# A two-layer graph network in rounds of gathers: x split beside its first product, degrees as bf16 products, filler by a load model

## The chip, the cores and the metric

The kernel runs on one core of one Trainium2 chip. Its time is the device time in microseconds (us) of one execution; the figure before is the median of three runs, 3415.57 us (3411.55 to 3430.43). One further execution was recorded by the hardware profiler; it took 2910.6 us, of which 2908.8 lie between the first and the last instruction of the trace (the span).

A core has five instruction streams: PE (TensorE, matmuls; its weight loads are listed as PEld), DVE (VectorE), ACT (ScalarE), POOL (GpSimd, used here to issue indirect gathers) and SP (SyncE, used here to issue all other transfers).

## The reference

12,500 nodes with 256 features each, 200,000 edges sorted by their target `dst`. Two convolutions take the mean over the incoming edges, then a linear layer, a residual and a layer norm:

```python
def _sage_conv(x, src, dst, W_l, b_l, W_r):
    msgs = x[src]
    agg = jax.ops.segment_sum(msgs, dst, num_segments=N_NODES)
    deg = jax.ops.segment_sum(jnp.ones((src.shape[0],), x.dtype), dst, num_segments=N_NODES)
    mean = agg / jnp.maximum(deg, 1.0)[:, None]
    return mean @ W_l + b_l + x @ W_r

h = jax.nn.relu(_sage_conv(x, src, dst, W1_l, b1, W1_r))
h = jax.nn.relu(_sage_conv(h, src, dst, W2_l, b2, W2_r))
x = _layernorm(x + h @ W3 + b3)
```

All in f32. `dst` is skewed: it is 12,500 times the square of a uniform number, so nodes with a low index have many edges and the later ones few.

## The kernel before

The nodes are cut into 98 blocks of 128. Each layer has two ways of summing over edges, and runs them beside each other.

**Hot nodes, by dense products.** The first nodes, in groups of 256 (5 groups in layer 1, 7 in layer 2), are not gathered. For each group `count` builds a matrix that says how often each of the 12,500 sources points to each of the 256 targets: bf16, 128 x 98 x 256. Per tile of 128 edges DVE makes the picks (L661) and, for four tiles, `low` (L665) and `aft` (L671); PE multiplies them (L691 for the first 128 tiles, L706 and L710 later), and DVE (L697) or ACT (L712) puts the result into `counts`. `product` (L628) then multiplies the matrix with x. x is kept as three bf16 parts whose sum is x; one load brings `rows`, the parts of two blocks (384 KB), and each block takes six matmuls (L638), 588 for a group. In layer 1 `degrees` (L728) also multiplies the counts by a column of ones. Counts made in layer 1 are written to HBM (`stored`) and read back in layer 2 (`loaded`).

**The split of x.** `split_rows` (L622) loads a block of x in f32 (`split_sb`, L833), `exact` makes the three parts (ACT casts L617 and L619, DVE subtractions L618 and L620, the last cast and difference written as bf16 `parts`), and a store puts them into `x3_d` in HBM (L626). The 98 splits run beside the count of group 0; the products of layer 1 read `x3_d` back.

**Cold edges, by rounds of gathers.** The other edges are taken in rounds of four tiles. Each round issues four indirect gathers on POOL (L243), 128 rows each, into one of four `got` buffers; DVE makes the selection matrices `one` (L201) and `two` (L207); PE multiplies them with the gathered rows (L254 into `part_ps`); ACT copies that out as `some` (L259); PE spreads it over 128 nodes (L265); DVE adds it (L277) to `sums`, a ring of eight blocks. In layer 1 the gathered rows carry a column of ones, so column 256 of `some` counts edges; a one-row f32 matmul (L270) spreads it and DVE adds it (L273) to `degs`, a ring too. Layer 1 has 186 groups of tiles, of which 83 take two rounds: 269 rounds with 1076 gathers. Layer 2 has 247 rounds with 988.

**Finished blocks.** When all edges of a block are summed, `first_block` (layer 1, three pieces) turns x (two transposes L839, ACT copy L842), makes the mean and the two products (`sage`, L863 and L865, DVE L868 and L869, ACT L871), clears its place in the rings (L894 for `sums`, L895 for `degs`), writes h to HBM (L896), splits h with `exact` and writes the parts (L899). The degrees of a block lie as a row of 128 numbers and are needed as a column: a matmul of that row with a single one (L886) turns it, the ACT copy takes it along, and DVE makes max and reciprocal (L889, L890). `last_block` (layer 2, five pieces) is the same with W3, residual and layer norm behind it.

**The order.** `layer` (L562) writes the order out by hand: per round one step of gathers, then three parts, each with at most one piece of a block and a share of the dense work, the filler. The filler is a generator that yields costs; `mixed` weaves the parts of a stage (a count, the product of the group before, a store) together and scales their costs to the largest plus 0.3 of the rest. Each round is given an equal share of the whole cost, until eight rounds before the end. The order on PE and POOL is this order; a scheduler sets that of DVE, ACT and SP from it.

The lines that set the share:

```python
        for i in range(i0, n + 1):
            before = gathers.step()
            due = dense_cost * min(1.0, (i + 1 - i0) / (n - i0 - 8))
            for part in range(3):
                ...
                pieces()
                fill(spent + (due - spent) / (3 - part))
```

Of the kernel before, what the change touches and what calls it, by code (L numbers as in the profile page):

```python
# [1 line left out]

# [19 lines left out]
P = 128  # L22
# [25 lines left out]
def by_runs(  # L48
# [79 lines left out]
    h3_d = dram.tile([P, NB, 3, D], BF16, name="h3_d")  # L128
    count_d = dram.tile([HG1 - 1, P, NB, DN], BF16, name="count_d")
# [86 lines left out]
    class Gathers:  # L216
# [45 lines left out]
        def summed(self, gr, some, two, done):  # L262
# [6 lines left out]
            if self.width > D:  # L269
                nc.tensor.matmul(sum_ps[0:1, NC], lhsT=some[:, D:D + 1], rhs=two,  # L270
                                 start=True, stop=True)
                deg = degs[:, bass.ds(n0, P)]
                nc.vector.tensor_add(deg, deg, sum_ps[0:1, NC])  # L273
# [288 lines left out]
    def layer(gathers, block, n_pieces, dense, dense_cost):  # L562
# [26 lines left out]
        filler = dense(waiting)  # L589
# [8 lines left out]
        begun = gathers.hot // P  # L598
        for i in range(i0, n + 1):
            before = gathers.step()  # L600
            due = dense_cost * min(1.0, (i + 1 - i0) / (n - i0 - 8))
            for part in range(3):
# [6 lines left out]
                fill(spent + (due - spent) / (3 - part))  # L609
# [11 lines left out]

    def split_rows(b):  # L622
        t = load_rows(x, N, b, "split_sb")
        s = work.tile([P, 3, D], BF16, name="parts")
        exact(t, s, t)
        nc.sync.dma_start(x3_d[:, b], s)  # L626

    def product(g, table3, c_sb):  # L628

        ps = dense_pool.tile([P, NC, DN], F32, name="dense_ps")  # L630
        nc.tensor.matmul(ps, lhsT=zeros_b, rhs=c_sb[:, :NC, :DN], start=True, stop=False)
        for b in range(NB):
            if b % 2 == 0:
                rows = work.tile([P, 2, 3, D], BF16, name="rows", bufs=3)
                nc.sync.dma_start(rows, table3[:, b:b + 2])
# [5 lines left out]
            yield COST_DENSE  # L641
# [4 lines left out]
    def count(g, to):  # L646
# [32 lines left out]
        for t in range(lo_g, highs[g]):  # L679
# [6 lines left out]
            if t < FIRST:  # L686
# [13 lines left out]
                yield count_cost(t)  # L700
            else:
                n0 = off_act.at(t)
                for a, b in halves:
# [10 lines left out]
                    yield count_cost(t) / len(halves)  # L714
# [7 lines left out]
    def degrees(g, c_sb):  # L722
# [3 lines left out]
        for j in range(DN // P):  # L726
            for b in range(NB):
                nc.tensor.matmul(ps[:, 0, j:j + 1], lhsT=c_sb[:, b, j * P:(j + 1) * P], rhs=ones_b,  # L728
                                 start=b == 0, stop=b == NB - 1)
                if b % 14 == 13:  # L730
                    yield COST_DEGREES
# [5 lines left out]
    COST_DENSE, COST_DEGREES, COST_SPLIT = 0.7, 1.6, 0.8  # L737
# [8 lines left out]
    def mixed(*parts):  # L746

        costs = [c for _, c in parts]
        scale = (max(costs) + 0.3 * (sum(costs) - max(costs))) / sum(costs)
        left = [[what, c, 0.0] for what, c in parts]  # L750
        while left:
            p = min(left, key=lambda p: p[2] / p[1])
            cost = next(p[0], None)
            if cost is None:
                left.remove(p)
            else:
                p[2] += cost
                yield cost * scale

    def stored(g, c_sb):  # L760
        for b0 in range(0, NB, 14):
            nc.sync.dma_start(count_d[g, :, b0:b0 + 14], c_sb[:, b0:b0 + 14, :DN])
            yield 0.5

    def loaded(g, c_sb):
        for b0 in range(0, NB, 14):
            nc.sync.dma_start(c_sb[:, b0:b0 + 14, :DN], count_d[g, :, b0:b0 + 14])
            yield 0.5

    def dense(g, table3, c_sb, waiting, with_deg):  # L770
        for p in product(g, table3, c_sb):
# [4 lines left out]
        if with_deg:  # L776
            yield from degrees(g, c_sb)
# [3 lines left out]
    def splits():  # L781
        for b in range(NB):
            split_rows(b)
            yield COST_SPLIT

    D_1 = NB * COST_DENSE + DN // P * (NB // 14) * COST_DEGREES
    D_2 = NB * COST_DENSE
    MOVED = NB // 14 * 0.5
    assert NB % 14 == 0 and HG == HG1 + 2

    def stages_1(waiting):

        for g in range(HG1 + 1):
            parts = [(count(g, counts[g % 2]), counting(g))]
            if g == 0:
                parts.append((splits(), NB * COST_SPLIT))
            else:
                parts.append((dense(g - 1, x3_d, counts[(g - 1) % 2], waiting, True), D_1))
                if g < HG1:
                    parts.append((stored(g - 1, counts[(g - 1) % 2]), MOVED))  # L800
            yield list(parts)

    def stages_2(waiting):

        order = [HG1 - 1, HG1, HG1 + 1, *range(HG1 - 1)]
        for i, g in enumerate(order):
            parts = [(dense(g, h3_d, counts[(HG1 - 1 + i) % 2], waiting, False), D_2)]
            if 1 <= i < HG - 1:
                n = order[i + 1]
                to = counts[(HG1 + i) % 2]  # L810
                parts.append((count(n, to), counting(n)) if n > HG1 else (loaded(n, to), MOVED))
            yield parts

    def staged(stages):
        def run(waiting):
            for parts in stages(waiting):
                yield from mixed(*parts)
        return run

    def cost_of(stages):  # L820
        whole = 0.0
        for parts in stages([]):
            costs = [c for _, c in parts]
            whole += max(costs) + 0.3 * (sum(costs) - max(costs))
        return whole
# [10 lines left out]
    def transposed(t, ps, name, more=0):  # L836

        for c in range(NC):
            nc.tensor.transpose(ps[:, c], t[:, c * P:(c + 1) * P], ident)  # L839
        s = work.tile([P, NC * P + 1], F32, name=name)  # L840
        n = NC * P + more
        nc.scalar.copy(s[:, :n], ps.rearrange("p c l -> p (c l)")[:, :n])  # L842
        return s[:, :NC * P].rearrange("p (c l) -> p c l", l=P), s[:, NC * P:]
# [34 lines left out]
    def first_block(b, agg=None):  # L878
        x_sb = load_rows(x, N, b, "x_sb")
        of_ring = agg is None  # L880
        yield True
        ps = turned()
        if of_ring:
            overlap(b, True)
            agg, deg_row = ring(b)
            nc.tensor.matmul(ps[:, NC, 0:1], lhsT=deg_row, rhs=ones[0:1, 0:1], start=True, stop=True)  # L886
        x_t, deg = transposed(x_sb, ps, "own_t", int(of_ring))
# [3 lines left out]
        yield True  # L891
# [426 lines left out]
```

## Time and profile before

| | before |
|---|---|
| median of 3 runs | 3415.57 us (3411.55 to 3430.43) |
| profiled execution | 2910.6 us |
| span of its trace | 2908.8 us |
| mean granted TensorE clock | 0.914 |
| dense products L638 on PE | 7056 matmuls, 976.9 us, 279 ns each |
| gathers L243 on POOL | 1076 and 988 |
| one-row degree products L270 | 186 |
| splits of x: load L833 to store L626 | 98 |
| loads of `rows` in layer 1 and 2 | 245 and 343, 384 KB each |
| HBM traffic | 582.80 MB read, 89.87 MB written |

The profiled execution is shorter than the runs that were timed, by a factor of 1.173. Profile and timed runs are therefore compared each with their own kind.

Engine rows of the profile give busy time, share of the span and number of instructions. Rows of groups give, for one line of the code, engine and shape, the number of instructions, the busy time and the mean of one in ns, then the engine's idle time just before them and what ended most of it. "issue" there is time in which the engine waited for nothing that the profile shows. L numbers are lines of the kernel before.

### The profile page before, as it was taken

What the parts mean: (1) busy time and instruction counts of PE and PEld (TensorE: products, weight loads), DVE (VectorE), ACT (ScalarE), POOL (GpSimd) and SP (SyncE); (2) the same over time, 40 slices, a digit from 0 to 9 for tenths busy, and PEclk for the clock granted to TensorE, in tenths of its full rate; (3) what the DMA queues carried; (4) which work ended last, traced back from release to release, by engine and by line L of the source; (5) the groups of instructions that cost most, each with busy time, mean ns of one, the idle gap of its engine ahead of it and who ended that gap; (6) DMA issues with size and microseconds to landing.
All of it is one profiled execution on the core that took longest, in us unless ns stands there. A gap on an engine that the chain in (4) does not pass through costs nothing.

```text
span 2908.8 us, 54100 instructions
## 1 busy us (share of the span) xinstructions
PE 2394.6 (82%) x18630; PEld 1632.6 (56%) x18630; DVE 1471.2 (51%) x4350; ACT 1253.6 (43%) x2702; POOL 2065.3 (71%) x2074
## 2 busy tenths in 40 slices
PE   3475755898998999999996677877889898899995
PEld 1132323565665666666764455555666666677774
DVE  6687764664554565566564124434323333444443
ACT  0422764675675676677673014444112122222222
POOL 5777764777777777777774777777777777777772
PEclk9676767998999999999998899889999999999998
DMA  4455668877877878767864677777989989888872
GB/s 124 128 174 164 198 188 271 260 232 235 277 228 247 273 227 292 248 215 225 251 203 124 214 246 231 219 220 230 296 284 305 299 287 291 276 265 266 266 251 71
DMA packets 408133, 676.44 MB, mean 233 GB/s; under 512 B 59659, under 2 KB 266537, under 8 KB 407849
## 3 DMA queue, kind: packets, MB, share of 16 engines
q1 hardware_dynamic: 303415, 400.51, 42.5%
q0 software_dynamic: 99072, 270.66, 30.5%
q8 instruction: 149, 2.44, 0.3%
q10 hardware_dynamic: 5362, 1.72, 0.3%
q14 instruction: 135, 1.11, 0.1%
HBM read 582.80 MB, written 89.87 MB: 231 GB/s over the span
## 4 chain that ended last, share of the span: by engine, by line
PE 54%; DMA 19%; POOL 8%; issue 7%; DVE 6%; ACT 4%; DVEq 0%; SPq 0%; ACTq 0%; POOLq 0%
PE dense_ps L638 19%; POOL got L243 8%; PE part_ps L254 7%; PE block_ps L863 6%; DMA got<-h_d,src_t 5%; PE count_ps L706 5%; PE block_ps L865 5%; PE sum_ps L265 4%; DMA x_sb<-in_x_dram 3%; DMA rows<-h_d 3%; DMA rows<-x_d 3%; PE block_ps L839 2%; PE block_ps L921 2%; DMA split_sb<-in_x_dram 2%; PE sum_ps L270 2%
## 5 line engine op out<-in xcount | busy, mean ns | idle before, releaser
L243 POOL DMA_INDIRECT got<-in_x_dram,src_t x1076 | 1116.7, 1038 | 446.5 <-issue 274.2
L243 POOL DMA_INDIRECT got<-h_d,src_t x988 | 946.4, 958 | 343.1 <-issue 285.3
L638 PE MATMUL dense_ps<-counts,rows 128*128 128x256 bf16 x7056 | 976.9, 279 | 51.3 <-DMA rows<-h_d 27.7
L712 ACT CAST counts<-count_ps 128x392 f32 (+2 forms) x1052 | 717.6, 682 | 290.2 <-PE count_ps L710 174.0
L638 PEld LDWEIGHTS <-rows 128*128 128x128 bf16 x7056 | 671.3, 100 | 287.5 <-issue 88.6
L254 PE MATMUL part_ps<-got,one 128*32 128x257 f32 (+1 forms) x4128 | 359.7, 422 | 192.1 <-DMA got<-h_d,src_t 123.0
L706 PE MATMUL count_ps<-pick,low 128*128 128x392 bf16 (+2 forms) x1052 | 343.4, 354 | 57.0 <-ACT counts L712 27.0
L661 DVE TENSOR_SCALAR pick<-steps,key_t 128x686 bf16<-128x686 f16 (+2 forms) x748 | 301.4, 413 | 127.6 <-PE count_ps L706 110.2
L201 DVE TENSOR_TENSOR one<-lo_t,lane_b 128x128 f32<-128x128 bf16 x516 | 149.1, 289 | 372.7 <-PE part_ps L254 370.5
L259 ACT COPY some<-part_ps 128x257 f32<-128x257 f32 (+1 forms) x361 | 136.1, 377 | 431.4 <-PE part_ps L254 428.2
L254 PEld LDWEIGHTS part_ps<-got,one 128*32 128x32 f32 x4128 | 85.9, 111 | 323.5 <-issue 176.4
L265 PE MATMUL sum_ps<-two,some 128*128 128x128 f32 x1444 | 238.2, 290 | 0.2 <-DVE sums L277 0.2
L265 PEld LDWEIGHTS sum_ps<-two,some 128*128 128x128 f32 x1444 | 205.0, 201 | 20.5 <-issue 8.7
L277 DVE TENSOR_TENSOR sums<-sums,sum_ps 128x256 f32 x361 | 148.4, 411 | 132.6 <-PE sum_ps L265 101.9
L868 DVE TENSOR_TENSOR own<-block_ps,biases 128x256 f32<-128x256 f32 x196 | 83.0, 423 | 230.9 <-PE block_ps L865 230.2
L706 PEld LDWEIGHTS <-low 128*128 128x128 bf16 x1052 | 101.8, 100 | 152.3 <-DVE pick L661 54.2
L842 ACT COPY own_t<-block_ps 128x256 f32<-128x256 f32 (+1 forms) x294 | 110.0, 375 | 123.7 <-PE block_ps L839 121.2
L871 ACT ACTIVATE h<-own 128x256 f32<-128x256 f32 x196 | 81.4, 415 | 179.3 <-DVE own L869 179.2
L665 DVE TENSOR_TENSOR low<-low_t,lane_b 128x512 bf16<-128x512 bf16 x187 | 127.9, 684 | 21.1 <-PE count_ps L710 20.5
L710 PE MATMUL count_ps<-aft,low 128*128 128x98 bf16 x614 | 131.9, 215 | 0.0
L863 PE MATMUL block_ps<-w1l_sb,sums 128*128 128x256 f32 x352 | 113.9, 452 | 2.1 <-DVE sums L277 1.8
L863 PE MATMUL block_ps<-w2l_sb,sums 128*128 128x256 f32 x336 | 104.1, 437 | 11.3 <-DVE sums L277 11.1
(180 smaller groups left out, 2495.1 us busy)
## 6 DMA issues: line engine op xcount, KB each, us to landing
rows<-h_d SPq DMA_DIRECT2D x343, 384.0 KB
rows<-x_d SPq DMA_DIRECT2D x245, 384.0 KB
count_d<-counts SPq DMA_DIRECT2D x28, 896.0 KB
counts<-count_d SPq DMA_DIRECT2D x28, 896.0 KB
x_sb<-in_x_dram SPq DMA_DIRECT2D x194, 128.0 KB
x_d<-parts SPq DMA_DIRECT2D x98, 192.0 KB
h_d<-parts SPq DMA_DIRECT2D x98, 192.0 KB
got<-in_x_dram,src_t POOLq DMA_INDIRECT x1076
```

What stands on the lines that cost most here:

```text
L201: nc.vector.tensor_tensor(one, lo[:, a:a + n * (G - 1) + 1:n].unsqueeze(2).to_broadcast([P, G, W]), lane_b[:, :W].unsqueeze(1).to_broadcas ...
L243: nc.gpsimd.indirect_dma_start(out=g[:, j, :D], out_offset=None, in_=self.table, in_offset=bass.IndirectOffsetOnAxis(ap=src_t[:, e:e + 1], ...
L254: nc.tensor.matmul(part_ps[j * W:(j + 1) * W, :width], lhsT=one[:, j], rhs=g[:, j, :width], start=r == 0, stop=r == n - 1)
L259: nc.scalar.copy(some[:, :width], part_ps[:, :width])
L265: nc.tensor.matmul(sum_ps[:, c], lhsT=some[:, c * P:(c + 1) * P], rhs=two, start=True, stop=True)
L277: nc.vector.tensor_add(own, own, sum_ps[:, :NC])
L638: nc.tensor.matmul(ps[:, c], lhsT=rows[:, b % 2, k, c * P:(c + 1) * P], rhs=c_sb[:, b, :DN], start=False, stop=b == NB - 1 and k == 2 and ...
L661: nc.vector.tensor_scalar(r[:, :w * NB], steps[:, :w * NB], key_t[g][:, t - lo_g:t - lo_g + 1], None, op0=OP.is_equal)
L706: nc.tensor.matmul(ps[:, :(b - a) * NB], lhsT=s, rhs=r[:, a * NB:b * NB], start=True, stop=alone)
L712: nc.scalar.copy(to[:, :, bass.ds(n0 + a, b - a)], ps[:, :(b - a) * NB].rearrange("p (d s) -> p s d", s=NB))
L863: nc.tensor.matmul(ps[:, 0], lhsT=agg[:, c], rhs=wl[:, c], start=c == 0, stop=c == NC - 1)
L865: nc.tensor.matmul(ps[:, 1], lhsT=own_t[:, c], rhs=wr[:, c], start=c == 0, stop=c == NC - 1)
```

## The change

1. **The split moves.** `product` no longer gets a table but a function that brings the rows of two blocks. For group 0 of layer 1 this is the new `split_rows`: it loads and splits two blocks of x straight into a `rows` buffer, writes them to `x3_d` with one store and hands the buffer to the product. The later groups of layer 1 and all of layer 2 use `loaded_rows`. In either case the rows of the next pair are brought one pair ahead (`following`). The 98 splits beside the count of group 0 go.
2. **Degrees of the cold edges as bf16.** The product L270 takes the upper half-words of its two f32 operands as bf16.
3. **Degrees turned through HBM.** The matmul L886 goes. `first_block` stores the row of degrees of a block in `deg_d` in its first piece and loads it back as a column in its second; max and reciprocal come in the third. `transposed` loses its extra column.
4. **Filler by a load model.** Generators now yield shares of their own whole instead of costs, and `in_turn` keeps the parts of a stage level. For every stage `of_count`, `OF_DENSE`, `OF_DEGREES` and `OF_SPLITS` give its load on PE, DVE and ACT; `base` gives what each round itself loads them with (its gathers' products and, smoothed over 12 rounds, the blocks it finishes). `paced` finds by bisection the length of a round at which all stages just fit under 0.95, 0.88 and 0.9 of the three engines, and from it how far the stages should have come after each round (`due`). `staged` runs the stages to there.

The core of the diff:

```diff
             if self.width > D:
-                nc.tensor.matmul(sum_ps[0:1, NC], lhsT=some[:, D:D + 1], rhs=two,
+
+                nc.tensor.matmul(sum_ps[0:1, NC], lhsT=some[:, D:D + 1].bitcast(BF16)[:, 1:2],
+                                 rhs=two.bitcast(BF16).rearrange("p (n h) -> p n h", h=2)[:, :, 1],
                                  start=True, stop=True)
...
+        upto = [left_after(g) if r == groups[g][1] - 1 else 0 for g, r in gathers.rounds]
+        upto = [max(begun, *upto[:i + 1], 0) for i in range(n)]
+        base = [[a + x / groups[g][1] + (upto[i] - upto[max(i - 12, 0)]) / 12 * y
+                 for a, x, y in zip((0.68, 0.29, 0.0), (0.7, 0.95, 0.38), of_block)]
+                for i, (g, r) in enumerate(gathers.rounds)]
+        due = paced(stages, base[i0:n - 8])
         for i in range(i0, n + 1):
             before = gathers.step()
-            due = dense_cost * min(1.0, (i + 1 - i0) / (n - i0 - 8))
+            upto = due[min(i - i0, len(due) - 1)]
...
-                fill(spent + (due - spent) / (3 - part))
+                fill(spent + (upto - spent) / (3 - part))
...
+    def loaded_rows(table3, b):
+        rows = work.tile([P, 2, 3, D], BF16, name="rows", bufs=3)
+        nc.sync.dma_start(rows, table3[:, b:b + 2])
+        return rows
+
     def split_rows(b):
-        t = load_rows(x, N, b, "split_sb")
-        s = work.tile([P, 3, D], BF16, name="parts")
-        exact(t, s, t)
-        nc.sync.dma_start(x3_d[:, b], s)
-
-    def product(g, table3, c_sb):
+
+        rows = work.tile([P, 2, 3, D], BF16, name="rows", bufs=3)
+        for k in range(2):
+            t = load_rows(x, N, b + k, "split_sb")
+            exact(t, rows[:, k], t)
+        nc.sync.dma_start(x3_d[:, b:b + 2], rows)
+        return rows
+
+    def product(g, rows_of, c_sb, whole):
...
+        following = rows_of(0)
         for b in range(NB):
             if b % 2 == 0:
-                rows = work.tile([P, 2, 3, D], BF16, name="rows", bufs=3)
-                nc.sync.dma_start(rows, table3[:, b:b + 2])
+                rows, following = following, rows_of(b + 2) if b + 2 < NB else None
...
-            yield COST_DENSE
+            yield COST_DENSE / whole
...
+    OF_DENSE = (NB * 0.7, 0.0, 0.6)
+    OF_DEGREES = (5.5, 0.0, 0.0)
+    OF_SPLITS = (0.0, NB * 0.82, NB * 0.75)
+    MOST_LOAD = (0.95, 0.88, 0.9)
+
     def stages_1(waiting):
 
         for g in range(HG1 + 1):
-            parts = [(count(g, counts[g % 2]), counting(g))]
-            if g == 0:
-                parts.append((splits(), NB * COST_SPLIT))
...
+            parts, loads = [count(g, counts[g % 2])], [of_count(g)]
+            if g:
+                parts.append(dense(g - 1, split_rows if g == 1 else partial(loaded_rows, x3_d),
+                                   counts[(g - 1) % 2], waiting, True))
+                loads += [OF_DENSE, OF_DEGREES] + [OF_SPLITS] * (g == 1)
+                if g < HG1:
+                    parts.append(stored(g - 1, counts[(g - 1) % 2]))
+            yield parts, loads
...
+        def by_rounds(length):
+            at, s = [], 0.0
+            for base in rounds:
+                left = 1.0
+                while s < len(loads) and left > 1e-9:
+                    of = loads[int(s)]
+                    speed = min((length * m - b) / f for m, b, f in zip(MOST_LOAD, base, of) if f)
+                    if speed <= 0:
+                        break
+                    step = min(speed * left, int(s) + 1 - s)
+                    left -= step / speed
+                    s = int(s) + 1 if step == int(s) + 1 - s else s + step
+                at.append(s)
+            return at
...
     def first_block(b, agg=None):
         x_sb = load_rows(x, N, b, "x_sb")
         of_ring = agg is None
-        yield True
-        ps = turned()
         if of_ring:
             overlap(b, True)
             agg, deg_row = ring(b)
-            nc.tensor.matmul(ps[:, NC, 0:1], lhsT=deg_row, rhs=ones[0:1, 0:1], start=True, stop=True)
-        x_t, deg = transposed(x_sb, ps, "own_t", int(of_ring))
+            nc.sync.dma_start(deg_d[b:b + 1], deg_row)
+        yield True
+        if of_ring:
+            deg = work.tile([P, 1], F32, name="deg")
+            with nc.allow_non_contiguous_dma(reason="a row becomes a column"):
+                nc.sync.dma_start(deg, deg_d[b, :, None])
+        x_t = transposed(x_sb, turned(), "own_t")
+        yield True
         if of_ring:
             nc.vector.tensor_scalar(deg, deg, 1.0, None, op0=OP.max)
             nc.vector.reciprocal(rdeg[:, b:b + 1], deg)
-        yield True
         h, own = sage(x_t, b, agg, w1l_sb, w1r_sb, biases[:, 0], "h")
...
-    layer(gathers_1, first_block, 3, staged(stages_1), cost_of(stages_1))
-    layer(Gathers(h_d, True), last_block, 5, staged(stages_2), cost_of(stages_2))
+    layer(gathers_1, first_block, 3, stages_1, (2.35, 2.0, 2.0))
+    layer(Gathers(h_d, True), last_block, 5, stages_2, (3.6, 2.6, 1.75))
```

## The prediction

> **What bounds the kernel now.** I read the engines' shares first, then the costliest groups, the idle time of the engine that looked steadiest, and last the stretches in which it stops.
>
> ```profile
> PE 2394.6 (82%) x18630; PEld 1632.6 (56%) x18630; DVE 1471.2 (51%) x4350; ACT 1253.6 (43%) x2702; POOL 2065.3 (71%) x2074
> ...
> L243 POOL DMA_INDIRECT got<-in_x_dram,src_t x1076 | 1116.7, 1038 | 446.5 <-issue 274.2
> L243 POOL DMA_INDIRECT got<-h_d,src_t x988 | 946.4, 958 | 343.1 <-issue 285.3
> ```
>
> PE looks like the bound at 82%, and POOL seems to have 29% to spare. The timeline of POOL says otherwise:
>
> ```profile
> 448.18 0.95 POOL L243 DMA_INDIRECT got<-in_x_dram,src_t  x1 [0.30 <-issue]
> 449.43 0.95 POOL L243 DMA_INDIRECT got<-in_x_dram,src_t  x1 [0.30 <-issue]
> 450.69 0.95 POOL L243 DMA_INDIRECT got<-in_x_dram,src_t  x1 [0.31 <-issue]
> 451.94 0.95 POOL L243 DMA_INDIRECT got<-in_x_dram,src_t  x1 [0.30 <-issue]
> 470.80 0.95 POOL L243 DMA_INDIRECT got<-in_x_dram,src_t  x1 [17.91 <-PE part_ps L254]
> ```
>
> Columns: start, duration, instruction, idle time before it and its releaser. Gathers follow each other every 1.25 us, and the 0.30 us between two is waited for by nothing: it belongs to the issue. So 2064 gathers need 2064 x 1.25 = 2580 of 2908.8 us. **POOL's issue is the bound**, about 5 us for a round of four. The rest: longer issues, (1.038-0.95) x 1076 = 95 us in layer 1 and 8 in layer 2; idle beyond 0.30 us, 446.5 - 323 - 22 at the start = 101 us in layer 1 and 343.1 - 296 - 32 = 15 in layer 2; 32 between the layers (1566 to 1598); some 25 before the first gather; 52 after the last. Only the idle parts can be won, and a gain on another engine counts only where POOL waits for it. Where POOL waits:
>
> ```profile
> 0.00:360.00 360.00, 259.21 (x231) 0.74 0.53 157
> 360.00:664.00 304.00, 192.46 (x187) 0.85 0.74 234
> 664.00:1566.00 902.00, 664.98 (x660) 0.96 0.76 241
> ```
>
> These are stretches with POOL's busy time, its gathers, the granted clock, the DMA share and GB/s. From 360 to 664 it is idle for 304 - 192.5 - 187 x 0.30 = 55 us beyond issue, from 664 to 1566 for 39. The first is where x is split and the first group's product begins:
>
> ```profile
> DVE split_sb L618 <- ACT parts L617: 53.8, 34, 5.9
> PEld block_ps L886 <- DVE own L869: 53.8, 6, 19.4
> PE block_ps L886 <- DVE own L869: 51.8, 6, 19.1
> POOL got L243 <- PE part_ps L254: 49.9, 10, 17.9
> ```
>
> This is who waited for whom from 371 to 543 (total, times, longest). VectorE stands behind split_sb operations whose data is late, L869 waits behind them in its queue, PE waits for L869, POOL for PE.
>
> **The split of x** (rounds 58 to 104). The 98 splits leave the count of group 0 and come into the product of group 0. By the instruction order, that product begins after 58 rounds of gathers, not 67, and runs to 104. 49 loads of rows (384 KB) fall away; casts and subtractions keep their number; 98 stores become 49 of twice the size. What changes is who waits: PE now multiplies directly what VectorE has just split. In the order of VectorE, the last subtraction of a pair stands level with the pair's first product or a round behind it, so there is no lead, and SP's order is: load one tile, store of the pair before (waits for VectorE), load the other tile. That is a loop of load, cast, subtraction, cast, subtraction, store. The trace shows its length before:
>
> ```profile
> 128.44 1.03 SPq L833 DMA_DIRECT2D split_sb<-in_x_dram  x2
> 132.47 0.75 ACT L617 CAST parts<-split_sb 128x256 bf16<-128x256 f32 x2 [5.23 <-DMA split_sb<-in_x_dram]
> 132.91 0.77 DVE L618 TENSOR_TENSOR split_sb<-split_sb,parts 128x256 f32<-128x256 f32 x2 [1.80 <-ACT parts L617]
> 133.43 0.71 ACT L619 CAST parts<-split_sb 128x256 bf16<-128x256 f32 x2
> 135.47 0.76 DVE L620 TENSOR_TENSOR parts<-split_sb,parts 128x256 bf16<-128x256 f32 x2
> 136.19 0.88 SPq L626 DMA_DIRECT2D x_d<-parts  x2
> 137.12 0.94 SPq L833 DMA_DIRECT2D split_sb<-in_x_dram  x2
> ```
>
> 8.7 us from load to load, 4.0 of them the load itself. Over the whole stretch, 96 loads from 118.6 to 532.1, a pair took 8.6 us. Lower end for the new loop: 4.0 + four operations of 0.42 + 0.45 to the store = 6.2. Upper end: 8.6 plus a third of a degree turn (below, 3.9) = 9.9. I take 8.0: one store issue less (0.4), a freer VectorE (204 of 255 us busy from 115 to 370, about half in the new loop), but a degree turn in every third pair. Then 47 pairs take 47 x 8.0 = 376 us. got has four buffers, so POOL runs up to three rounds ahead before it feels this, and PE catches up later: less 15, 361 us. Before, the same 187 gathers took 304. **Cost 57 us** (ends: 276 and 450, so -28 and +146). The count of group 0 without splits, rounds 15 to 58, I leave at its time: POOL hardly waited there, and the long issues, seen where picks are dense, move with the picks.
>
> **bf16 degree product** (L270). In a saturated stretch it starts 0.31 us before the next matmul; L728, bf16 too, takes 0.03 for one column, so some 0.06 is left. 186 x 0.25 = 46 us of PE. **Degrees turned through HBM**: L886 goes, 88 x 0.31 = 27 us of PE. Its wait on L869 does not: it is a wait for the block_ps buffer, which the transposes (L839) need just as well. Added are 88 stores and 88 loads on SP, 0.32 us to issue each. The load waits until the store has landed, and on SP the next x, split and rows loads queue behind it; on ACT the clearing of degs (L895) waits for the store too, ahead of count copies. Nearest rows: a whole h block to HBM 1.69 us, x_sb back 2.25, together 3.9. [...] Off the path where rows are loaded ahead; on it in the split loop (counted) and at the end of layer 1.
>
> **The load model.** It moves dense work, counts and degrees between rounds. From 1100 to 1500 PE is busy for 391 of 400 us, and a round takes 5.5 us (72.5 rounds in this stretch). By the order, about 21 dense matmuls a round late in layer 1 become 15, and 19 at the end of layer 2 become 12; at some 0.12 us each (starts of one after another) the six fewer are 0.7 us a round, and the lighter degrees 0.2 more. PE then needs less than POOL's 5 us, but POOL's pace stays. Of 39 us I take **25 as gain** (ends 0 and 39; rows DMAs end some of these waits). In layer 2, of 15, **5** (0 to 15). Between the layers, the last two blocks of group 4, which took 1586 to 1595, now come before the last gather (order); less the degree turn: **4** (-4 to 9). The 52 at the end hold the same blocks: 0.
>
> **Sum** against the profiled execution (2908.8 span, 2910.6 with what lies around it): +57 - 25 - 5 - 4 = +23, **2934 us, 0.8% more**. The runs shown have a median of 3415.57, 1.173 times as long; the page does not show why. In proportion that gives 3443. [...] I take 3440, nearer to the plain proportion.
>
> **Rivals.** (1) The loop keeps near 6.2 us: 276 - 304 - 34 = -62, 2849, in proportion 3343. For it: VectorE is freer, and rows has three buffers. Against: the measured mean was 8.6 with two tiles in flight, and the order shows no lead. (2) The longer runs are long because PE is slow in them (granted 0.91 here, 0.78 would stretch PE alone as much). Then 73 us less PE work and even rounds count fully, about 3.5%: 3295. Against: nothing shows a lower clock. (3) SP's queue decides: from a loop of 9 us on, each degree turn holds the next split load; at 9.9 us it is +146 - 10, 3046, in proportion 3575. For: one queue carries it all. Against: only each third pair has a turn. (4) Loss and gain cancel: 3415.
>
> Chances: forecast 0.40, rival 3 0.12 (both slower), rival 1 0.26, rival 2 0.08 (faster), rival 4 0.14. So slower by over 0.5% (about what a measurement here can tell) 0.52, within 0.14, faster 0.34. Range 3335 to 3540: a loop from 6.1 to 9.6 us; the forecast's own, 7.6 to 8.9, is 3420 to 3495.
>
> **What will show it.** Right: between rounds 58 and 104 POOL waits over 100 us for part_ps, twelve dense matmuls come in bursts some 8 us apart, and PE waits for split casts and subtractions; after that gathers step by 1.25 us almost without gaps; L270 starts under 0.1 us before its follower. Wrong: dense bursts every 5 us, or gaps in POOL after rows loads held up behind deg loads. The whole falls if POOL's step is no longer 1.25 us.

## The result, and the profile after

The changed kernel takes **3586.38 us** (median, 3580.88 to 3593.63) against 3413.56 for the kernel before (3401.66 to 3430.43): **1.0504 times** as long, 95% interval 1.0455 to 1.0553. Its profiled execution took 3593.63 us, with a span of 3591.8.

One fact has to come first, since the numbers can't be read without it: chips differ. The experiments came to five. On three of them, **chips A**, the kernel before takes 2901 to 2907 us; on two, **chips B**, 3384 and 3414. On either kind its profile is as long as its timed runs there (before_again below, 2914.9 us profiled and a median of 2906.8 timed; before_slow, 3374.6 and 3379.8), so I take the profile of before (2910.6 us) and the timed runs (3413) to come from different chips. The result was measured where before takes 3414. On chips A the same change costs 0.7%.

The page of the changed kernel (a chip where before takes 3414), the rows that answer to those of before:

```profile
PE 2610.4 (73%) x18268; PEld 1704.1 (47%) x18268; DVE 1464.5 (41%) x4350; ACT 1250.3 (35%) x2702; POOL 2028.6 (56%) x2074
...
L245 POOL DMA_INDIRECT got<-in_x_dram,src_t x1076 | 1083.2, 1007 | 842.5 <-PE part_ps L256 274.7
L245 POOL DMA_INDIRECT got<-h_d,src_t x988 | 943.2, 955 | 661.6 <-issue 283.5
```

A gather is issued as fast as before (means of 1007 and 955 ns; 1038 and 958 before), but POOL's idle time has nearly doubled (1504 us; 790 before), and in layer 1 the largest part of it ends with PE's product of gathered rows. POOL is no longer the bound: it waits for PE to hand back `got` buffers. By stages (rounds 0 to 58, 58 to 104, the rest of layer 1, layer 2), POOL's busy time, gathers, granted clock, DMA share and GB/s, first the changed kernel, then the kernel before, profiled later on a chip B (before_slow below):

```profile
0.00:389.00 389.00, 246.37 (x242) 0.79 0.36 103
389.00:787.00 398.00, 188.30 (x185) 0.74 0.53 165
787.00:1929.00 1142.00, 650.70 (x660) 0.86 0.63 193
1964.00:3534.00 1570.00, 943.23 (x988) 0.88 0.67 208
```

```profile
0.00:396.00 396.00, 258.81 (x243) 0.75 0.49 144
396.00:726.00 330.00, 190.61 (x185) 0.81 0.69 214
726.00:1773.00 1047.00, 658.57 (x660) 0.91 0.67 207
1811.00:3315.00 1504.00, 943.84 (x988) 0.89 0.70 217
```

Less busy time and 0.30 us of issue for each gather, POOL waits 70, 154, 293 and 330 us in the changed kernel, and 64, 84, 190 and 264 in the one before. So the loss on chips B lies in three places: some 70 us where x is split, 100 in the rest of layer 1 and 65 in layer 2 (the two chips differ by 30 us in all). On a chip A the changed kernel (after_3 below) reads:

```profile
0.00:355.00 355.00, 255.24 (x242) 0.87 0.40 113
355.00:690.00 335.00, 185.15 (x185) 0.81 0.63 196
690.00:1583.00 893.00, 663.81 (x660) 0.95 0.79 247
1610.00:2881.00 1271.00, 944.35 (x988) 0.96 0.81 257
```

There the waits are 27, 94, 31 and 30 us, against 31, 55, 39 and 15 in the profile that the prediction worked from: the split has grown by 39, layer 2 by 15. Who waited for whom in rounds 58 to 104 of the changed kernel, on the chip of the result (total, times, longest):

```profile
POOL got L245 <- PE part_ps L256: 106.9, 19, 10.8
...
PE dense_ps L657 <- ACT rows L630: 49.6, 33, 11.4
PE dense_ps L657 <- ACT rows L628: 49.1, 26, 9.8
```

PE stands before the casts of the rows it is about to multiply, and POOL behind PE.

### The profile page after: what moved, and what is told of

Read it like the earlier page. It is cut to its first block, busy times and chain, and to the rows that moved or that the text cites. A ratio compares the mean times of both kernels' runs of the same rounds, so it can differ in the third digit from the quotient of the medians.

```text
span 3591.8 us, 53609 instructions
## 1 busy us (share of the span) xinstructions
PE 2610.4 (73%) x18268; PEld 1704.1 (47%) x18268; DVE 1464.5 (41%) x4350; ACT 1250.3 (35%) x2702; POOL 2028.6 (56%) x2074
## 4 chain that ended last, share of the span: by engine, by line
PE 57%; issue 12%; another core or an unknown queue 10%; DVE 7%; DMA 7%; ACT 5%; POOL 1%; SPq 1%; DVEq 0%; ACTq 0%; POOLq 0%
PE dense_ps L657 19%; PE part_ps L256 8%; PE block_ps L914 6%; PE count_ps L725 6%; PE block_ps L916 5%; PE sum_ps L267 4%; DMA rows<-h_d 4%; PE block_ps L975 2%; ACT counts L731 2%; PE block_ps L891 2%; PE count_ps L729 1%; DMA split_sb<-in_x_dram 1%; DVE pick L680 1%; PE dense_ps L747 1%
## 5 line engine op out<-in xcount | busy, mean ns | idle before, releaser
L245 POOL DMA_INDIRECT got<-in_x_dram,src_t x1076 | 1083.2, 1007 | 842.5 <-PE part_ps L256 274.7
L657 PE MATMUL dense_ps<-counts,rows 128*128 128x256 bf16 x7056 | 1063.3, 294 | 260.0 <-DMA rows<-h_d 79.1
L657 PEld LDWEIGHTS <-rows 128*128 128x128 bf16 x7056 | 690.9, 104 | 593.5 <-issue 163.3
L725 PE MATMUL count_ps<-pick,low 128*128 128x392 bf16 (+2 forms) x1052 | 374.5, 380 | 182.6 <-ACT counts L731 76.0
L256 PE MATMUL part_ps<-got,one 128*32 128x257 f32 (+1 forms) x4128 | 399.4, 447 | 76.3 <-issue 32.6
L267 PE MATMUL sum_ps<-two,some 128*128 128x128 f32 x1444 | 255.4, 305 | 12.5 <-DVE sums L281 5.4
L267 PEld LDWEIGHTS sum_ps<-two,some 128*128 128x128 f32 x1444 | 223.7, 216 | 49.0 <-issue 26.7
L893 ACT COPY own_t<-block_ps 128x256 f32<-128x256 f32 x294 | 110.0, 376 | 290.3 <-PE block_ps L891 95.0
L256 PEld LDWEIGHTS part_ps<-got,one 128*32 128x32 f32 x4128 | 91.3, 115 | 231.0 <-issue 174.5
L914 PE MATMUL block_ps<-w1l_sb,sums 128*128 128x256 f32 x352 | 128.1, 498 | 70.8 <-DVE sums L281 52.3
L891 PE MATMUL block_ps<-ident,h 128*128 128x128 f32 x196 | 45.4, 317 | 130.0 <-ACT h L922 72.8
```

The lines of the kernel that those rows point to most:

```text
L245: nc.gpsimd.indirect_dma_start(out=g[:, j, :D], out_offset=None, in_=self.table, in_offset=bass.IndirectOffsetOnAxis(ap=src_t[:, e:e + 1], ...
L256: nc.tensor.matmul(part_ps[j * W:(j + 1) * W, :width], lhsT=one[:, j], rhs=g[:, j, :width], start=r == 0, stop=r == n - 1)
L267: nc.tensor.matmul(sum_ps[:, c], lhsT=some[:, c * P:(c + 1) * P], rhs=two, start=True, stop=True)
L657: nc.tensor.matmul(ps[:, c], lhsT=rows[:, b % 2, k, c * P:(c + 1) * P], rhs=c_sb[:, b, :DN], start=False, stop=b == NB - 1 and k == 2 and ...
L725: nc.tensor.matmul(ps[:, :(b - a) * NB], lhsT=s, rhs=r[:, a * NB:b * NB], start=True, stop=alone)
L914: nc.tensor.matmul(ps[:, 0], lhsT=agg[:, c], rhs=wl[:, c], start=c == 0, stop=c == NC - 1)
```

## The experiments

Each kernel is compared with the kernel before on its own chip. "S" is the move of the split, "L" the pace of the load model (`paced`), "B" the bf16 degree products, "T" the turns through HBM. Beside the kernel before itself, only_split and lumpy_before are made from it; all others are made from the changed kernel and keep `in_turn`. All of them but lumpy_before bring rows one pair ahead.

### One part back at a time, on a chip A

**before_again**: the kernel before, unchanged.

> The kernel before, unchanged, to get a profile of an execution as long as those that are timed. Theory 'split' (the loss lies where x is split and multiplied): this profile spends 300 to 330 us in rounds 60 to 104 where the changed kernel spends 385, and the two keep the same pace (6.0 to 6.6 us a round) elsewhere. Theory 'schedule' (the load model sets PE waiting in all stages): this profile is faster by 2 to 5% in layer 2 as well (1569 us from first to last gather in the changed kernel). Theory 'other state': the span is again near 2910 and the timed runs differ from any profile.

1.0016 [0.9996, 1.0036], span 2913.0: the first profile again, on a chip where the timed runs lie there too (2901). So that profile is true to its chip, and the question is what differs between the chips.

**split_back** (L, B, T; the splits are a part of stage 0 again and products read `x3_d`):

```diff
+            if g == 0:
+                parts.append(splits())
+                loads += [OF_SPLITS]
...
-                parts.append(dense(g - 1, split_rows if g == 1 else partial(loaded_rows, x3_d),
+                parts.append(dense(g - 1, partial(loaded_rows, x3_d),
```

> The changed kernel with the 98 splits back beside the count of group 0 and read again from x3_d, the rest as changed. Theory 'split': near 3430 us, within 1% of before. Theory 'schedule': stays above 3530. Theory 'SP queue' (degree turns hold up the row loads): 3500 to 3560, since the turns stay.

2871.83 us, 0.9895 [0.9866, 0.9925]: the rest of the change, taken together, is a gain here. Rounds 58 to 104 take 269.8 us (POOL's row):

```profile
357.50:627.30 269.80, 187.64 (x185) 0.83 0.79 246
```

**even_fill** (S, B, T; `paced` gives each round the same share of the old costs, with the old length of each stage):

```diff
-        loads = [[sum(x) for x in zip(*l)] for _, l in stages([])]
+        costs = [old_cost(stages, i) for i in range(len(list(stages([]))))]
...
+            c = ends[-1] * (i + 1) / len(rounds)
```

> The changed kernel with the load model replaced by the even share of the old costs per round (x still split in the product of group 0, degrees still turned through HBM). Theory 'schedule': back to 3400 to 3460 us. Theory 'split': stays at 3560 to 3640, or longer, since the product of group 0 then gets fewer rounds than the model gave it. Theory 'SP queue': 3570 to 3600.

2960.09 us, 1.0205 [1.0171, 1.024]. It is slower than the changed kernel proves to be on a chip A (after_3): the model's pace helps there.

**turn_back** (S, L, B; `first_block` as before, with the matmul):

```diff
-            nc.sync.dma_start(deg_d[b:b + 1], deg_row)
+            nc.tensor.matmul(ps[:, NC, 0:1], lhsT=deg_row, rhs=ones[0:1, 0:1], start=True, stop=True)
```

> The changed kernel with the degrees turned by the matmul again (no deg_d), the rest as changed. Theory 'SP queue': 3430 to 3500 us. Theories 'split' and 'schedule': 3570 to 3610, within 1% of the changed kernel, the 27 us of matmul on PE against it.

2939.95 us, 1.0136 [1.0096, 1.0176]. With the matmul it is no faster than the changed kernel (1.0073 in after_3): on chips A the turns through HBM show no cost, and SP's queue doesn't decide.

**after_3**: the changed kernel on another chip A.

> The changed kernel once more. On the chip where before takes 2900 us: 2925 to 2960, 1.01 to 1.02 times before, from turn_back (2940) and even_fill (2960), which each have three of its four changes, and split_back (2872), which lacks the move of the split. On the chip where before takes 3410: 3580 to 3600 again.

2931.21 us, **1.0073** [1.0054, 1.0091]. The split costs 1.0073 against 0.9895, 1.8%; its 46 rounds take 334.6 us against 269.8.

### On a chip B

**after_again**: the changed kernel.

> The changed kernel, unchanged, on the chip that the experiments share with the kernel before. Theory 'split' with a chip-dependent size: where before takes 2900 us, this takes 2925 to 2960 (1.01 to 1.02 times), since turn_back and even_fill lay there; where before takes 3410 it takes 3580 again. Theory 'the ratio is the kernel's own': 1.045 to 1.055 times before wherever it runs.

3595.01 us, 1.0516 [1.0478, 1.0553]: the ratio belongs to the chip.

**two_ahead** (rows split two pairs ahead of their product):

```diff
-        following = rows_of(0)
+        ahead = 2 if rows_of is split_rows else 1
+        following = [rows_of(2 * i) for i in range(ahead)]
```

> The changed kernel with rows split two pairs ahead of their product in group 0 (three rows buffers as they are). If the split loop is long because nothing is split ahead (latency of load, cast, subtraction, cast, subtraction in the path): 25 to 70 us less than the changed kernel, the loop 6.5 to 7.5 us a pair. If it is limited by what VectorE, ACT and the load queue get through, or by the order in which they stand behind other work: within 10 us of the changed kernel.

3581.75 us, 1.0472 [1.0434, 1.0511]. 13 us less, between the two expectations. Rounds 58 to 104 take 377.1 us in place of 396.5, and rounds 104 to 269 give it back (1144.8 against 1126.8). More lead in the order is not what the kernel lacks.

**only_split** (S alone on the kernel before):

```diff
-            if g == 0:
-                parts.append((splits(), NB * COST_SPLIT))
-            else:
+            if g:
...
+        bring = split_rows if first else lambda b: loaded_rows(table3, b)
+        following = bring(0)
```

> The kernel before with the split of x moved into the product of group 0 and nothing else (f32 degrees, matmul turns, even filler). Theory 'split': slower than before by 50 to 110 us (split_back, which has all but this, was 29 faster than before, and even_fill 59 slower). Theory 'parts lean on each other' (only together with the load model or the turns does the split cost): within 30 us of before.

3479.52 us, 1.0183 [1.0155, 1.021]: +66 us, the same 1.8% as on chips A.

**split_turn_back** (L and B: the edits of split_back and turn_back together):

> The kernel before with the load model and the bf16 degree products alone: splits beside the count of group 0, degrees turned by the matmul. If the turn through HBM is worth its saving on PE, this is slower than split_back by some 10 to 25 us; if SP's queue pays for it, faster by 5 to 20; the gathers' pace alone would leave the two within 10 us.

3538.33 us, 1.0373 [1.0345, 1.0402]. The expectation compared it with split_back, which has no run on a chip B, so it says nothing on T. What it does say came as a surprise: split_back, which has T besides, had gained 1% on a chip A; this costs 3.7% here.

**before_slow** (the kernel before), **deg_only_slow** (B and T: the edits of split_back and even_fill together) and **even_fill_slow** (S, B, T, as even_fill), on the other chip B:

> The kernel before once more, for a profile where it takes 3410 us. Theory 'PE is late there because what it has done is seen late': POOL issues a gather a median of 1 to 2 us after the product that frees its buffer, against 0.38 where before takes 2900, and its rounds take 6.0 us at the least, the heavier ones more; with the even share fewer of its rounds are above 6.5 us than with the load model.

> split_back_even once more: the kernel before with the degree changes alone. It was 0.995 times before where before takes 2900 us. Where before takes 3410: theory 'the load model is what costs there' 0.985 to 1.005 times before, 'the degree turns on SP cost there' 1.02 to 1.04.

> even_fill once more: the changed kernel with the old even share of dense work. It was 1.0205 times before where before takes 2900 us, the changed kernel 1.007. Where before takes 3410: theory 'the load model is what costs there' 1.01 to 1.03 times before (3450 to 3510 us), about as only_split, against 1.05 of the changed kernel; theory 'everything costs more there' 1.05 to 1.08.

deg_only_slow is 1.0319 [1.0273, 1.0364] and even_fill_slow 1.0522 [1.0474, 1.057] times before. So the load model's pace, which I had blamed, is not the cost: without it the loss is just as large (1.0522 against 1.0516 of after_again). But deg_only_slow is slower in layer 2 too, where no degrees are made. Layer 2 in three stretches (rounds 269 to 352, 352 to 478, 478 to the end), POOL's rows, the kernel before and then deg_only_slow, on one chip:

```profile
1811.00:2314.50 503.50, 320.08 (x332) 0.83 0.61 186
2314.50:3081.60 767.10, 479.46 (x505) 0.91 0.77 240
3081.60:3315.00 233.40, 144.30 (x152) 0.94 0.66 206
```

```profile
1879.40:2382.50 503.10, 319.78 (x333) 0.83 0.61 186
2382.50:3199.10 816.60, 479.42 (x504) 0.89 0.73 225
3199.10:3433.00 233.90, 144.97 (x152) 0.93 0.67 208
```

The first and third are alike within 0.5 us; the second is 49.5 longer. (deg_only_slow also asks for rows one pair ahead; only_split does so too, and its second stretch took 774.5 us.) In these rounds, and in no others of layer 2, counts are loaded beside a product. `in_turn` counts each of a stage's parts alike: seven loads together weigh as much as 98 blocks of products. So each load uses up the share of up to two rounds, in which no product is issued, and then products come at double rate: in lumps. Dense matmuls in rounds 391 to 410, counted in PE's order in the traces of before_slow and after_3:

```
before   18 18 18 18 24 18 12 24 18 18 18 18 18 24 18 12 24 18 18 18
changed  42 30  0  0 36 42  0  0 30 36 18  0  6 36 36  6  0 18 36 30
```

In layer 2 the mean is 17 in both; the standard deviation is 4.1 before and 12.7 after. The stores of counts in layer 1 do the same (this is in the changed kernel, whatever its pace, and in deg_only_slow and even_fill_slow).

### Why chips B feel it, and what their rounds wait for

**light_2** and **light_slow**: layer 2 with hardly any dense work: products over two blocks of 98, no counts.

```diff
-            parts = [dense(g, partial(loaded_rows, h3_d), counts[(HG1 - 1 + i) % 2], waiting, False)]
+            parts = [dense(g, partial(loaded_rows, h3_d), counts[(HG1 - 1 + i) % 2], waiting, False, 2)]
...
-                parts.append(count(n, to) if n > HG1 else loaded(n, to))
```

> The changed kernel with most of layer 2's dense work left out: each group's product takes two blocks of the 98, and the counts of layer 2 are neither made nor read back, so its output is not the reference's. Layer 1 is whole. What is read is the time from first to last gather of layer 2, 247 rounds. If the gathers themselves are slower on the chip where before takes 3410 us, it is 1480 to 1510 us there (6.0 us a round, as in the lightest rounds of after_again); if PE's work and its waits set those 6 us, it falls to 1240 to 1260, four issues of 1.25 us a round, as where before takes 2900.

> light_2 once more (layer 2's products over two blocks of 98, no counts there, so its output is not the reference's). Where before takes 2900 us it took 1242 us from first to last gather of layer 2. Where before takes 3410: 1240 to 1260 if PE's load and its late releases set the 6 us of a round there, 1480 to 1510 if the gathers are slower there. The changed kernel takes 1574 there.

From the first gather of layer 2 to the last, light_2 took 1242 us on a chip A, light_slow 1468 on a chip B. Neither theory holds: PE, with 784 us busy in 1469, still doesn't let the rounds fall to 5 us, and the gathers are not slower (0.95 us each; a median of 2.4 us from issue to landing, by the packets in the trace; in layer 2 of the full kernels, with 48 packets in order to each gather, 3.6 us in the first profile of before and 3.3 in that of the result). What is longer is the time from PE's end of a product to the start of those who wait for it. Three engines that wait for one product, in light_slow:

```profile
2592.78 0.64 PE L256 MATMUL part_ps<-got,one 128*32 128x256 f32 x8 [0.60 <-DMA got<-h_d,src_t]
2593.35 0.44 PE L890 MATMUL block_ps<-ident,h_sb 128*128 128x128 f32 x2
2609.47 0.29 DVE L203 TENSOR_TENSOR one<-lo_t,lane_b 128x128 f32<-128x128 bf16 x1 [4.42 <-remote]
2609.53 0.37 ACT L261 COPY some<-part_ps 128x256 f32<-128x256 f32 x1 [6.38 <-remote]
2609.70 0.94 POOL L245 DMA_INDIRECT got<-h_d,src_t  x1 [2.34 <-remote]
2609.95 1.08 PE L256 MATMUL part_ps<-got,one 128*32 128x256 f32 x8 [16.16 <-ACT some L261]
```

PE has ended the product L256 by 2593.4. It frees a buffer of `one` for DVE and one of `got` for POOL, and its result is what ACT copies. All three start 16 us later, within 0.3 us of each other, and PE then waits for the copy. (They had other work in between, so their own idle times are shorter.) "remote" means that the profile found no releaser. The same in numbers: where POOL had to wait more than 0.8 us for a buffer, it issued a median of 0.38 us after the end of the product that frees it on chips A (0.38 at the 10th percentile, 0.39 at the 90th, 42 rounds of after_3). On chips B the median was 1.26 us in after_again (344 rounds) and 2.33 in before_slow (353), and 5.2 at the 90th percentile in both; the 10th is 0.38 there too.

Ends of matmuls are modelled, on both alike, so PE might in truth end late. But it mostly doesn't stand still: where ACT's copy came over 2 us after the product's end (92 times in after_again), PE had started a median of 12 more matmuls by then. A hand-over that PE has no part in is not longer: from DVE's `own` to ACT's `h` it is a median of 0.03 us in after_3 and after_again. And a lower granted clock alone doesn't explain it. PE's rows for layer 2 of light_2 on a chip A and of light_slow on a chip B:

```profile
1620.00:2863.00 1243.00, 747.79 (x4255) 0.77 0.46 136
1933.00:3402.00 1469.00, 783.67 (x4197) 0.73 0.39 115
```

At a clock of 0.77 a chip A still issues its rounds in 5 us each (1243 us for 247), while before_slow at 0.89 takes 6 (1504).

A product of gathered rows ends a median of 12 us after its gather was issued in layer 2 of after_3 and 23 us in after_again: nearly four rounds, all the buffers that there are. On chips A, where four rounds take 20 us, some 8 us are then in hand against a lump. On chips B, where four rounds of the changed kernel take 25 us (1570 us for 247), some 2 are left. Both are estimates from these medians, and that this slack decides is argued from them; no run changed the number of buffers.

### The lumps alone, and without them

**lumpy_before** (the kernel before, every part weighing the same), **smooth** (the changed kernel, stores and loads weighing little), **smooth_split_back** (that, and the splits back in stage 0). The edits:

```diff
-                yield cost * scale
+                yield cost / p[1] * sum(costs) * scale / len(costs)
```

```diff
-        left = [[what, 0.0] for what in parts]
+        left = [[what, 0.0, 0.02 if what.__name__ in ("stored", "loaded") else 1.0] for what in parts]
+        whole = sum(p[2] for p in left)
...
-                yield share / len(parts)
+                yield share * p[2] / whole
```

> The kernel before with one edit in mixed: every part of a stage counts for the same share, as in in_turn, so that the stores and loads of counts push the dense work into lumps; the length of each stage is kept, and split and degrees are as before. Standard deviation of dense matmuls per round in layer 2: 12.0 in place of 4.1. Theory 'lumps': 1.02 to 1.035 times before where before takes 3400 us, 1.003 to 1.012 where it takes 2900. Theory 'the degrees cost it': within 0.005 of before on either.

> The changed kernel with one edit in in_turn: a stored or loaded part counts for 0.02 of a product or a count when shares are given out, not for as much as they do. By the order of instructions layer 2's dense matmuls per round then have a standard deviation of 5.1 (none without any), where the changed kernel has 12.7 (43 rounds without, 18 with 40 or more) and the kernel before 4.1. Theory 'lumps' (what costs is that the dense work comes in lumps of four to five rounds): where before takes 3400 us, 1.005 to 1.025 times before in place of 1.051, about what only_split costs (1.018); where before takes 2900, 0.995 to 1.003 in place of 1.007. Theory 'the degrees cost it': still 1.04 to 1.055 where before takes 3400.

> smooth with the splits back beside the count of group 0, the version that should beat both. Theory 'lumps': 0.985 to 1.005 times before where before takes 3400 us, 0.978 to 0.988 where it takes 2900 (split_back, with the lumps, 0.9895). Theory 'the degrees cost it': 1.02 to 1.035 where before takes 3400.

These ran on a chip A, and none of them on a chip B. lumpy_before: 2944.83 us, 1.0148 [1.0116, 1.018], more than expected. smooth: 2896.03 us, 0.997 [0.9952, 0.9987], 1.0% better than the changed kernel. smooth_split_back: **2831.69 us, 0.9754** [0.9721, 0.9787], the fastest of all, and better than expected. Of its page, the first row:

```profile
PE 2316.3 (82%) x18268; PEld 1598.7 (56%) x18268; DVE 1459.2 (51%) x4350; ACT 1243.5 (44%) x2702; POOL 2063.7 (73%) x2074
```

POOL's 2063.7 us and 0.30 us of issue for each of 2064 gathers are 95% of the span of 2836.7: hardly a wait is left for another engine to give up.

**split_back_even** (the kernel of deg_only_slow on a chip A):

> The kernel before with the two changes to the degrees alone: bf16 degree products and turns through HBM; x split beside the count of group 0, dense work at the old even share per round. Where before takes 2900 us: 2870 to 2900, on either side of split_back (2872), which has the load model too. Where before takes 3410: theory 'the load model costs 120 us there' (split_turn_back with it and the bf16 products was 124 slower than before) says 3380 to 3420, 100 to 150 below the kernels that have the load model; theory 'the degrees cost it' says 3500 to 3540.

2894.01 us, 0.9951 [0.9932, 0.997].

What the runs show together: the split costs 1.8% on either kind of chip (by removal on A, alone on B), and 2.2% between the two smooth kernels. On chips A the lumps cost 1.0 to 1.5%. On chips B the split alone costs 66 us (only_split) and the rest without the load model's pace 107 (deg_only_slow), as much together as the changed kernel's 173, though on different chips. Of the 107, the lumps cost 50 us in layer 2. The 61 us that deg_only_slow loses in rounds 104 to 269 of layer 1 (1107.4 against 1046.3) come from the lumps or from the degree changes, and the traces point to the lumps: 45 of them lie in rounds 104 to 222, where counts are stored beside a product, 0.38 us a round against 0.39 in the lumpy stretch of layer 2; and in these rounds split_turn_back, which has no turns through HBM (but the model's pace), took 837 us where before_slow took 752. A run that would show it, lumpy_before or smooth on a chip B, is missing. Why PE's results are seen late on chips B stays open. The traces of chips B also hold fewer than half the semaphore events (27,651 for before_slow, 68,154 for before_again; 29,273 in the profile of the result, 68,138 in the first of before); whether the two have one cause isn't shown.

## Why the prediction was wrong

**The step that failed** is the load model's term, "Of 39 us I take **25 as gain**" and "In layer 2, of 15, **5**", and its transfer to the longer runs: "The runs shown have a median of 3415.57, 1.173 times as long; the page does not show why. In proportion that gives 3443." There the split was sized right: 57 us, 67 in proportion, and 66 alone in only_split. The rest of the change was to win 34 us, 40 in proportion, and cost 107 (deg_only_slow), so that +27 became +173. "PE then needs less than POOL's 5 us" holds for the mean of ten rounds ("about 21 dense matmuls a round late in layer 1 become 15"); round by round the order goes from 0 to 48 of them in layer 2. And where the runs take 3414 POOL's pace doesn't cover that: POOL waits for PE in two rounds of three (344 of 516 in after_again).

**Where the sum seems right, luck has a part.** Made against the profiled execution it was 2934 us and +0.8%; the changed kernel takes 2931 and +0.7% on chips A. Between the two profiles the split stretch gave +33 where I had +57, and layer 2 +12 where I had -5.

**Rivals.** Rival 3 came nearest with 3575, but for a wrong reason: it put 146 us into the split stretch, by degree turns. On the chip of the result that stretch grew by 68, and layer 2, which has no degree turns, by 66. Rival 2 had the right suspicion, a PE that sets the pace of the long runs; but its cause, the clock, does not explain them by itself (light_2 kept rounds of 5 us at 0.77; light_slow took 6 at 0.73, before_slow 6 at 0.89), and it drew a gain of 3.5% from it, since it too counted averages. Nor do the instructions of VectorE and POOL take longer on chips B. DVE's `own`, before_again on a chip A and before_slow on a chip B:

```profile
L869 DVE SCALAR_TENSOR_TENSOR own<-block_ps,rdeg,own 128x256 f32<-128x256 f32 x196 | 94.0, 480 | 4.1
L869 DVE SCALAR_TENSOR_TENSOR own<-block_ps,rdeg,own 128x256 f32<-128x256 f32 x196 | 94.2, 481 | 4.1
```

The other large groups of DVE agree within 2% (picks 412 and 408 ns, `one` 288 and 287), and a gather of layer 2 takes a mean of 956 ns in after_3 and in before_slow. So it is not by longer operations there that the runs on chips B take 16 to 23% more.

Point by point, on chips A:

- *Split, +57 us.* The 46 rounds took 335 us, and a pair's products began every 7.0 us, where I had 361 and 8.0. Against the same rounds of before (302) that is +33. But split_back shows 270 without the split: the stall that I saw in before's profile there would have gone with the rest of the change. Measured so, the split costs 65 us in these rounds, and 1.8% or 52 us in all. Right in size, by two errors that cancel. PE waits for casts, as foretold; POOL waits 69 us for part_ps on a chip A and 107 on the chip of the result, where over 100 was foretold.
- *Load model and PE savings, -25 in layer 1, -5 in layer 2.* After round 104 layer 1 took 892 us in place of 901, rounds 0 to 58 took 329 for 336, and layer 2 lost 12 us instead of winning 5. smooth shows the part that the lumps ate: layer 2 in 1251 us, 6 less than before.
- *bf16 degrees.* From the start of L270 to its follower: a median of 0.31 us before, in two passes (372 matmuls in the trace for 186 products), and 0.15 in one after (186); 0.16 us saved and not 0.25.
- *Turn through HBM.* Added at no cost that shows: turn_back, without it, is no faster (1.0136 against 1.0073). The sum had charged it in every third pair of the split. Rival 3 (SP's queue decides) falls on chips A with that; on chips B no pair of kernels differs in T alone.
- *Between the layers, -4.* 1583.0 to 1610.6, 27.6 us for 31.9: right.

## What to carry to other kernels

Read a schedule round by round, not by its mean: a generator that is to keep parts level must weigh them by the time they take, and a part of few steps that cost PE nothing (seven loads beside 98 products) must weigh almost nothing (0.02 in smooth). Ask how many of the buffers between a steady engine and a lumpy one are in use before you call a lump free: here a product ended a median of 12 us after its gather on chips A, where four buffers last 20, and 23 on chips B, where they last 25; that this decides is argued, not shown. And when the profile's own time is far from the runs' median, don't carry a sum over by proportion: first find out which engine waits for which in the longer ones.

## What was not expected of the hardware

Two chips of five took 16 to 23% longer for the same kernel, with the same durations of single instructions on DVE and POOL (`own` 480 and 481 ns, a gather 956 on both). The mean granted clock is lower there too (before: 0.92 and 0.87; the changed kernel: 0.92 and 0.84), but light_2 kept its rounds of 5 us at 0.77 on a chip A. What differs most of the times compared here is the time from PE's end of a product to the start of who waits for it: for POOL 0.38 us against a median of 1.3 to 2.3, and 16 us in the case above. So the order of two versions can turn: one and the same kernel took 0.9951 times as long as before on a chip A (split_back_even) and 1.0319 on a chip B (deg_only_slow).
